# A 0/1 mask for GpSimd: one-byte floats in place of two-byte ones, in a graph attention stack

## The chip, the cores and the metric

The kernel runs on one core of a Trainium2 chip. The metric is the device time of one execution in microseconds (us); the time of a kernel is the median of its runs. In the profile, PE is TensorE (PEld its weight load), DVE is VectorE, ACT is ScalarE, POOL is GpSimd, and SP issues the DMAs.

## The reference

The input is x of 16 graphs x 1024 nodes x 128 features, in float32, and one adjacency matrix of 1024 x 1024 integers for all graphs. Three layers of masked multi-head attention (8 heads of 16) with a feed-forward part follow each other, then one layer in which the score of an edge is a leaky sum of two node values:

```python
def gnn(adj, h, ...):                                # layers 0, 1, 2
    Q, K, V = (h @ Wq), (h @ Wk), (h @ Wv)           # 8 heads of 16
    scores = einsum('bnhd,bmhd->bhnm', Q, K) / sqrt(16)
    scores = where(adj == 0, -inf, scores)
    x = h + einsum('bhnm,bmhd->bnhd', softmax(scores), V) @ Wo + bo
    x = layer_norm(x)
    return layer_norm(x + relu(x @ W1 + b1) @ W2 + b2)

def last(x, adj, ...):                               # layer 3
    h = x @ W
    e = leaky_relu((h @ a_src)[:, :, None] + (h @ a_dst)[:, None, :], 0.2)
    att = nan_to_num(softmax(where(adj == 0, -inf, e)))
    return layer_norm(att @ h + x)
```

## The kernel before

**Blocks and steps.** One block is one graph in one of the three attention layers, 48 in all; graphs go through the layers in groups of four. A block has 32 steps: two groups `g` of four heads, two halves `qh` of 512 query nodes, eight tiles `kt` of 128 key nodes. A step makes the scores of four heads for 128 keys x 512 queries, with keys on the partitions. It takes them in two pairs of heads (`pp` 0 and 1): for each pair PE writes 128 x 1024 scores into a PSUM slot (three slots in all, `s`; L422).

**Two ways to mask.** The scores of a pair become masked exponentials in a tile `e` (six in all) in one of two ways. On the first, ACT takes the exponential from PSUM (L429) and POOL multiplies the result in SBUF, in place, by the 0/1 mask `mask01` (L430). On the second, DVE adds `mask_add`, which holds 0 or -57344 in one-byte floats, to the scores in PSUM (L432), and ACT takes the exponential of that later, in place (L444). The first way is used for the first pair of the steps with `kt` not in (2, 5, 7), so for 5 of 8 steps, 960 times in all; all other pairs, 2112, go the second way.

```python
on_pool = pp == 0 and kt not in BOTH_ON_DVE
m = (mask01 if on_pool else mask_add)[:, kt, q0:q0 + 512][:, None, :].to_broadcast([P, 2, 512])
if on_pool:
    nc.scalar.activation(ev, psv, AF.Exp, scale=HD ** -0.5)
    behind["pool"] = nc.gpsimd.tensor_mul(ev, ev, m).ins
else:
    behind["dve"] = nc.vector.tensor_add(ev, psv, m).ins
```

**Sums.** Four steps later (`AHEAD`) PE multiplies the exponentials by the values, with a column of ones for the sum (L449, eight matmul records a step, into one PSUM accumulator `acc`). After the eight steps of a half, DVE transposes the accumulator (L460) and POOL scales it (L463).

**Around the steps.** Between the steps PE, ACT and DVE work on the next block's projections and on the last block's output projection, feed-forward part and layer norms. POOL has the rest of a layer norm: the small operations on the means and variances (L336 to L338), the scaling of each row tile (L340), gain and bias (L344, L345). The order of PE and ACT is written out by hand, that of DVE and POOL in the main loop comes from the planner of the framework; each engine goes through its list in order and waits on semaphores.

**The masks.** At the start the adjacency rows arrive by DMA as integers, DVE turns them into 0/1 bf16 (L196), PE transposes them into PSUM as bf16 (L202), and `masks()` makes both masks from there: DVE copies to `mask01` (L207), ACT makes `mask_add` (L208). There are eight row tiles. Four are done before the first step, and four in steps 1 to 4, in which the order of DVE is by hand as well.

**The last layer.** For each graph it runs beside later blocks. It reads `mask01` too: in `edges()` DVE takes the maximum of PSUM with 1 and multiplies by the mask in one instruction (L609), 128 times.

## Time and profile before

| | |
|---|---|
| time, median of 3 runs | 4011.02 us (4008.79 to 4011.72) |
| span of the profiled execution | 4007.5 us |
| its time beside the span | not listed apart |
| PE busy | 3767.4 us, 94% |
| DVE busy | 3412.3 us, 85% |
| ACT busy | 3380.2 us, 84% |
| POOL busy | 3450.1 us, 86% |
| mean granted TensorE clock | 0.983 |

A share of busy time is an average over stages. The steady part runs to about 3840 us; each block of attention takes about 73 us there when no last layer runs beside it. The last 150 us are the end of the last graph, with POOL and ACT mostly idle. In the rows of the profile, the number after x counts instructions, then come busy time and mean ns of one, then the idle time of the engine just before them and what ended it. A wait named after a releaser is inferred from semaphore events.

### The profile page before, as it was taken

How to read it: one execution, taken by the hardware profiler on the slowest of the kernel's cores; microseconds unless marked ns; L12 is line 12 of the kernel's file. 1: busy time of each engine (PE TensorE's matmuls, PEld its weight loads, DVE VectorE, ACT ScalarE, POOL GpSimd, SP SyncE). 2: the span in 40 equal slices, each digit the busy share in tenths (PEclk: the TensorE clock that was granted, in tenths of full speed). 3: DMA queues.
4: the chain of work that ended last, by engine and by line, in shares of the span. 5: the costliest groups of instructions: out<-in, count | busy, mean ns of one | idle time of the engine just before them, and what ended most of it. 6: DMA issues, size and time to landing. Idle time of an engine off the chain costs nothing.

```text
span 4007.5 us, 107755 instructions
## 1 busy us (share of the span) xinstructions
PE 3767.4 (94%) x44501; PEld 1551.0 (39%) x44501; DVE 3412.3 (85%) x5326; ACT 3380.2 (84%) x3961; POOL 3450.1 (86%) x3010
## 2 busy tenths in 40 slices
PE   7999999999999999999999999999999999999986
PEld 2333333344443333334444333333444433333435
DVE  7888988988888988988888988988888898988864
ACT  7999999977779999997777999999777799999850
POOL 5889989988889989998788999989888899989884
PEclk8999999999999999999999999999999999999998
DMA  6222122212222222122222222222222121222100
GB/s 162 64 65 59 49 64 65 53 46 67 55 56 59 56 64 64 48 60 55 55 55 55 64 64 57 51 64 65 55 55 55 49 64 49 59 65 62 46 7 20
DMA packets 124465, 233.13 MB, mean 58 GB/s; under 512 B 34624, under 2 KB 73792, under 8 KB 123968
## 3 DMA queue, kind: packets, MB, share of 16 engines
q1 hardware_dynamic: 122960, 225.71, 22.5%
q8 instruction: 354, 5.80, 0.6%
q14 instruction: 143, 1.17, 0.1%
q10 hardware_dynamic: 1008, 0.44, 0.0%
HBM read 15.54 MB, written 8.39 MB: 6 GB/s over the span
## 4 chain that ended last, share of the span: by engine, by line
PE 60%; DVE 17%; POOL 16%; issue 4%; ACT 3%; SPq 1%; DMA 0%; ACTq 0%; DVEq 0%; POOLq 0%
PE acc L449 23%; PE t L296 19%; PE s L422 15%; DVE e L432 10%; POOL e L430 7%; POOL x L344 3%; POOL x L345 3%; DVE st L321 3%; PE t L285 2%; POOL mv L338 1%; DVE x L328 1%; ACT e L444 1%; DVE lo L385 1%; DVE mv L323 1%; POOL x L340 1%
## 5 line engine op out<-in xcount | busy, mean ns | idle before, releaser
L432 DVE TENSOR_TENSOR e<-s,mask_add 128x1024 f32<-128x1024 f32 x2112 | 2492.6, 1213 | 315.1 <-PE s L422 206.5
L444 ACT ACTIVATE e<-e 128x1024 f32<-128x1024 f32 x2112 | 2193.6, 1062 | 197.5 <-DVE e L432 181.6
L430 POOL TENSOR_TENSOR e<-e,mask 128x1024 f32<-128x1024 f32 x960 | 2052.9, 2152 | 343.4 <-ACT e L429 326.9
L449 PE MATMUL acc<-e,v 128*17 128x512 f32 x12288 | 1636.2, 604 | 61.9 <-POOL e L430 30.4
L422 PE MATMUL s<-Wq,Wk 64*128 64x512 f32 x6144 | 1177.0, 455 | 50.1 <-DVE e L432 33.6
L429 ACT ACTIVATE e<-s 128x1024 f32<-128x1024 f32 x960 | 982.9, 1024 | 245.9 <-PE s L422 245.8
L422 PEld LDWEIGHTS s<-Wq,Wk 64*128 64x128 f32 x6144 | 499.3, 186 | 1011.1 <-issue 397.5
L449 PEld LDWEIGHTS acc<-e,v 128*17 128x17 f32 x12288 | 208.0, 95 | 574.1 <-issue 466.9
L340 POOL TENSOR_SCALAR x<-x,mv 128x128 f32<-128x128 f32 x896 | 389.1, 448 | 23.5
L296 PE MATMUL t<-hd,e 128*32 128x129 f32 x8192 | 243.5, 276 | 5.7 <-DVE x L624 3.3
L338 POOL TENSOR_TENSOR mv<-mv,half_neg 128x4 f32<-128x4 f32 x224 | 232.5, 1038 | 18.6
L344 POOL TENSOR_TENSOR x<-x,ln_g 128x1024 f32<-128x1024 f32 (+1 forms) x97 | 229.6, 2367 | 10.3 <-PE t L285 6.3
L296 PEld LDWEIGHTS t<-hd,e 128*32 128x32 f32 x8192 | 226.3, 111 | 23.9 <-DVE lo L385 9.9
L328 DVE TENSOR_TENSOR x<-t,x 128x512 f32<-128x512 f32 x192 | 131.5, 685 | 93.5 <-PE t L296 93.5
L296 PE MATMUL t<-x1T,W 128*32 128x512 f32 x1536 | 200.1, 592 | 1.9 <-DVE x L624 1.0
L321 DVE BATCH_NORM_STATS2 st<-x 128x6 f32<-128x128 f32 x896 | 197.0, 279 | 3.3
L296 PEld LDWEIGHTS t<-W,hT 128*32 128x32 f32 x6144 | 174.0, 111 | 59.9 <-issue 45.5
L296 PE MATMUL t<-W,hT 128*32 128x128 f32 x6144 | 188.1, 275 | 1.8 <-ACT x1T L290 0.9
L285 PEld LDWEIGHTS t<-identf,x 128*128 128x128 f32 x888 | 95.8, 142 | 227.6 <-issue 87.5
L285 PE MATMUL t<-identf,x 128*128 128x128 f32 x888 | 156.0, 291 | 27.0 <-DVE parts L586 7.4
L385 DVE TENSOR_TENSOR lo<-t,hi 128x512 fp32r<-128x512 f32 x188 | 128.2, 682 | 35.6 <-ACT hi L384 35.6
L336 POOL TENSOR_SCALAR mv<-mv 128x4 f32<-128x4 f32 x224 | 53.0, 236 | 122.6 <-DVE mv L323 102.7
(97 smaller groups left out, 2507.7 us busy)
## 6 DMA issues: line engine op xcount, KB each, us to landing
Wk<-hi SPq DMA_DIRECT2D x384, 128.0 KB
Wk<-lo SPq DMA_DIRECT2D x384, 128.0 KB
Wq<-hi SPq DMA_DIRECT2D x384, 128.0 KB
Wq<-lo SPq DMA_DIRECT2D x384, 128.0 KB
x<-in_x_dram SPq DMA_DIRECT2D x16, 512.0 KB
out_dram<-x SPq DMA_DIRECT2D x31, 256.0 KB
ai<-in_adj_dram SPq DMA_DIRECT2D x8, 512.0 KB
g_rows<-parts SPq DMA_DIRECT2D x120, 4.0 KB
```

Of the source, the lines that this page charges most:

```text
L285: nc.tensor.transpose(ps[:, t * P:(t + 1) * P], src[:, 4 * h + t, :], identf)
L296: nc.tensor.matmul(dst[j:j + SLOT, :], lhsT[:, j:j + SLOT], rhs, start=start, stop=stop)
L321: nc.vector.bn_stats(st[:, t, :], z[:, t, :])
L338: nc.gpsimd.tensor_tensor(v, v, half_neg[:, ts], OP.pow)
L340: nc.gpsimd.tensor_scalar(z[:, t, :], z[:, t, :], mv[:, t, 0:1], mv[:, t, 1:2], op0=OP.add, op1=OP.mult)
L344: nc.gpsimd.tensor_mul(z, z, rows(gain, n))
L422: nc.tensor.matmul(ps[:, r * 512:(r + 1) * 512], k[64 * r:64 * r + 64, kt * P:(kt + 1) * P], q[64 * r:64 * r + 64, q0:q0 + 512], start=Tru ...
L429: nc.scalar.activation(ev, psv, AF.Exp, scale=HD ** -0.5)
L430: behind["pool"] = nc.gpsimd.tensor_mul(ev, ev, m).ins
L432: behind["dve"] = nc.vector.tensor_add(ev, psv, m).ins
L444: nc.scalar.activation(ev, ev, AF.Exp, scale=HD ** -0.5)
L449: nc.tensor.matmul(acc[j * SLOT:j * SLOT + HD + 1, :], v_bufs[m % 2][:, kt, 2 * j + g, :], e[:, j, :], start=first, stop=last)
```

## The change

`mask01` is allocated as `float8e5` (the type that `mask_add` has already) in place of bf16, 8 KB instead of 16 KB on each partition; 0 and 1 are exact in both. The copy that fills it gets the flag for a conversion without saturation. The instructions, their order on each engine and the sizes of all pools are the same.

```diff
-    mask01 = const.tile([P, NT, N], BF16)
+    mask01 = const.tile([P, NT, N], F8W)
     mask_add = const.tile([P, NT, N], F8W)
...
     def masks(t, ps):
         psv = ps.rearrange("p (k q) -> p k q", q=P)
-        nc.vector.tensor_copy(mask01[:, :, t * P:(t + 1) * P], psv)
+        nc.vector.tensor_copy(mask01[:, :, t * P:(t + 1) * P], psv, saturate=False)
```

The instructions that touch `mask01` are L207 (8 times, DVE), L430 (960 times, POOL) and L609 (128 times, DVE).

## The prediction

> **What bounds the kernel now.** First the page's busy times, then the windows of two stages (for each engine: busy us, and instructions in brackets).

> ```profile
> PE 3767.4 (94%) x44501; PEld 1551.0 (39%) x44501; DVE 3412.3 (85%) x5326; ACT 3380.2 (84%) x3961; POOL 3450.1 (86%) x3010
> ```

> ```profile
> 418.00:752.00 334.00, 320.94 (x3276) 117.02 (x3278) 298.41 (x437) 315.20 (x358) 305.01 (x260) 1.00 0.23 58
> 1753.00:2086.00 333.00, 315.97 (x4432) 148.06 (x4431) 280.26 (x471) 255.42 (x320) 277.42 (x253) 0.98 0.22 56
> ```

> PE is busy for 321 of 334 us in a stage of attention layers and 316 of 333 where the last layer is mixed in. So PE sets the pace in both. POOL, where the edit lands, has 29 and 56 us free. What counts is how its queue meets PE's, so next the groups of POOL and DVE (count | busy us, mean ns | idle before).

> ```profile
> L430 POOL TENSOR_TENSOR e<-e,mask 128x1024 f32<-128x1024 f32 x960 | 2052.9, 2152 | 343.4 <-ACT e L429 326.9 <-DMA Wk<-lo 11.1 <-DMA ln_gamma<-in_L_gnn_ln_gamma_dram 1.4
> L340 POOL TENSOR_SCALAR x<-x,mv 128x128 f32<-128x128 f32 x896 | 389.1, 448 | 23.5
> L344 POOL TENSOR_TENSOR x<-x,ln_g 128x1024 f32<-128x1024 f32 x95 | 227.1, 2390 | 9.8 <-PE t L285 5.8
> L463 POOL TENSOR_TENSOR A<-tt,recs 128x256 f32<-128x256 f32 x192 | 119.7, 624 | 1.5 <-DVE recs L462 1.5
> L336 POOL TENSOR_SCALAR mv<-mv 128x4 f32<-128x4 f32 x224 | 53.0, 236 | 122.6 <-DVE mv L323 102.7 <-DVE chk L352 4.5
> ...
> L344 POOL TENSOR_TENSOR x<-x,ln_gamma 128x512 f32<-128x512 f32 x32 | 41.1, 1284 | 1.9
> ```

> ```profile
> L432 DVE TENSOR_TENSOR e<-s,mask_add 128x1024 f32<-128x1024 f32 x2112 | 2492.6, 1213 | 315.1 <-PE s L422 206.5 <-ACT e L444 97.6 <-ACT hT L505 0.7
> ...
> L609 DVE SCALAR_TENSOR_TENSOR e<-s,mask 128x1024 f32<-128x1024 f32 x128 | 150.4, 1212 | 4.2 <-PE s L606 3.5
> ...
> L207 DVE COPY mask<-s 128x1024 bf16<-128x1024 bf16 x8 | 5.5, 690 | 4.8 <-PE s L202 4.5
> ```

> The edit touches L430, L609 and L207. Who waits for L430: the list of waits (us in total, times, longest), and one such place in the timeline.

> ```profile
> PEld acc L449 <- POOL e L430: 43.8, 33, 4.5
> ...
> PE acc L449 <- POOL e L430: 30.4, 16, 4.2
> ```

> ```profile
> 1003.29 2.38 POOL L345 TENSOR_TENSOR x<-x,ln_b_last 128x1024 f32<-128x1024 f32 x1
> 1005.62 2.13 POOL L430 TENSOR_TENSOR e<-e,mask 128x1024 f32<-128x1024 f32 x1
> ...
> 1007.81 1.05 PE L449 MATMUL acc<-e,v 128*17 128x512 f32 x8 [2.94 <-POOL e L430]
> ```

> PE itself stands still for L430 only 30.4 us in all. In the place shown, four scale-and-shift instructions precede the one multiplication that PE wants. Over the timeline I set the end of each of the 960 multiplications against the start of its step's L449: the median slack is 4.2 us, a quarter have under 3.4, 57 under 1, 11 under 0.1.

> [...]

> **The change part by part.** No instruction, wait or transfer is added or moved, on any queue; 8 KB a partition come free and no buffer count uses them.

> *L430.* No row of POOL shows a one-byte operand. Fixed cost from the fp32 pair: 1284 - 512 x 2.16 = 178 ns. Per element then: fp32 with fp32 2.16 ns, fp32 with bf16 (2152-178)/1024 = 1.93, fp32 with a scalar repeated 16 times (L463) (624-178)/256 = 1.74. Counted in four-byte words read per element these are 2, 1.5 and 1.06, so a word costs 0.44 to 0.46 ns. With one byte it is 1.25 words: 1.93 - 0.25 x 0.45 = 1.81 ns, 2.04 us in all. That is the value I take, -0.11 us, 106 us less POOL busy. Lower end: the rate of one input, (448-236)/124 = 1.71 ns, gives 1.93 us (-0.22). Upper end: one-byte conversion may cost extra; the nearest price is the fp32 row, 2.39 us (+0.24), and nothing in the profile excludes more.

> What a change d of each is worth in time I work out from the timeline: POOL's lag grows by d with each multiplication, shrinks by its idle time before one that waited for ACT (201 times), and where it exceeds the slack above, PE and all behind it move by the rest; a gain counts only as far as PE really stood still. Result:

> - d = -0.22: -4 us; -0.11: -2.6
> - d = +0.10: +4; +0.12: +7
> - d = +0.24: +56; +0.32: +101; +0.50: +225

> The gain is small because one to three multiplications lie between POOL's last idle time and each stall. The loss is steep because POOL has 29 us for 91 multiplications in the attention stage, 0.32 us each; above d = 0.32 POOL bounds it.

> *L609.* L432 already reads a one-byte mask_add beside PSUM in 1213 ns, L609 a bf16 mask in 1212. Cost: none, both ends within 0.02 us x 128 = 2.6 us.

> *L207.* [...]+0.52 us x 8 = 4.2 us on DVE, and ACT's L208 starts after it. The first four end before 19 us, where PE waits until 24.7 for the DMA of Wq anyway. Of the other four, most go into gaps such as this one, 0.47 of 0.52:

> ```profile
> 35.67 0.69 DVE L207 COPY mask<-s 128x1024 bf16<-128x1024 bf16 x1 [1.13 <-PE s L202]
> ...
> 36.83 1.23 DVE L432 TENSOR_TENSOR e<-s,mask_add 128x1024 f32<-128x1024 f32 x1 [0.47 <-PE s L422]
> ```

> I take +1 us, ends 0 and 4.2; if the cover is gone, all 4.2 show.

> *Sum.* Span 4007.5 - 2.6 + 0 + 1 = 4005.9. The profile gives no total beside the span; the median 4011.0 stands 3.5 above it. Forecast 4009.5, -0.04%, inside the 0.2% (8 us) that a measurement can tell from no change.

> **The rivals.** (1) *POOL pays for one byte.* Place: L430, 960 times; price +0.24 us or more; it decides from 2.27 us on (+0.12, +8 us with L207). At the fp32 price the time is 4011 + 56 + 1 = 4068; at +0.5, 4237. For it: POOL's rate does depend on the type, and one byte is unseen. Against it: the three rates above order by bytes read, the fewer the faster.
> (2) *The gain is on the path.* The chain gives L430 7.2% of the span, 288 us, some 134 multiplications; x 0.11 is -15 us, 3997 with L207. Against it: in the pattern that repeats every block the chain reaches PE through "POOL mv L338" (ended at 494.51 us in one), where DVE's L460, which frees the accumulator, ended at 494.46. There PE waits for L460, not for POOL.
> (3) *Nothing changes on POOL*[...]: 4011 + 1 = 4012, as good as the forecast.

> **How the numbers follow.** Forecast with (3), d between -0.22 and about +0.10: 0.54, own range 4003 to 4017. (1): 0.38, high because nothing measured here excludes it. (2): 0.08. The faster chance is (2), the slower (1). From 4003, some 5% are left below; upward the range takes in the fp32 price and a little (d = 0.28, +80), 4090, leaving about 15% of (1) above.

> **What would show it.** In the changed profile: L430's mean (2.04 right, 2.15 for (3), 2.27 or more for (1)); POOL busy near 3340; PE's wait on L430 within a few us of 30.4 (over 60 means (1)); L207 near 1.2 us; L609 at 1.21. Wrong would be an L430 of unchanged or lower mean with a time over 8 us away: then the slack is misread.

## The result, and the profile after

The changed kernel takes 4003.0 us (median of 13 runs, 4000.31 to 4007.38), the kernel before beside it 4011.7 us (13 runs, 4008.79 to 4018.69). The ratio is 0.998, 95% interval 0.9972 to 0.9988: 8.7 us less. Repeated later with 21 runs it was 4003.97 us and 0.9983 (0.9976 to 0.9989). So the gain is real, though it is just at the 8 us that the prediction took for what a measurement can tell from no change. The time lies 6.5 us below the forecast of 4009.5, at the very lower end of the stated range of 4003 to 4090. The instructions first: busy times, and the chain's shares by engine, from the page of the changed kernel:

```profile
span 4003.6 us, 107755 instructions
PE 3763.0 (94%) x44501; PEld 1552.2 (39%) x44501; DVE 3415.6 (85%) x5326; ACT 3379.7 (84%) x3961; POOL 3333.5 (83%) x3010
PE 64%; DVE 19%; POOL 8%; ACT 5%; issue 3%; SPq 0%; DMA 0%; ACTq 0%; DVEq 0%; POOLq 0%
```

The groups of the edited instructions and of L432 (count | busy us, mean ns | idle before):

```profile
L430 POOL TENSOR_TENSOR e<-e,mask 128x1024 f32<-128x1024 f32 x960 | 1935.7, 2027 | 436.2 <-ACT e L429 436.0
...
L432 DVE TENSOR_TENSOR e<-s,mask_add 128x1024 f32<-128x1024 f32 x2112 | 2492.4, 1213 | 305.5 <-PE s L422 187.2 <-ACT e L444 96.6 <-POOL e L430 8.3
L609 DVE SCALAR_TENSOR_TENSOR e<-s,mask 128x1024 f32<-128x1024 f32 x128 | 150.4, 1212 | 3.6 <-PE s L606 3.1
L207 DVE CAST mask<-s 128x1024 fp8e5<-128x1024 bf16 x8 | 9.8, 1222 | 4.6 <-PE s L202 4.5
```

L430 went from 2152 to 2027 ns, and POOL is busy for 116.6 us less. L609 is unchanged. L207 is now called a CAST and takes 1222 ns instead of 690. All of this is close to what the prediction worked out. Who waits for L430 (us in total, times, longest), from the waits of the changed kernel:

```profile
PEld acc L449 <- POOL e L430: 58.6, 90, 4.0
...
PE acc L449 <- DVE tt L460: 28.3, 50, 1.0
PE acc L449 <- POOL e L430: 23.1, 11, 3.7
PE acc L449 <- POOL x L340: 7.7, 32, 0.3
```

And two of these rows in the kernel before:

```profile
PE acc L449 <- POOL mv L338: 18.2, 32, 0.6
PE acc L449 <- DVE tt L460: 10.5, 40, 0.6
```

PE waits 7.3 us less for L430. But its wait for L460 grew from 10.5 to 28.3 us, and the row of "POOL mv L338" is gone. Most of it is one wait under two names. Set place by place, the 32 waits for L338, 18.2 us in all, are in the changed kernel waits of 18.3 us for L460, and six waits for L430 of 6.0 us in all are six of 6.0 us for L460. One of these is at 1041.6 us, where the kernel before shows a pause of 1.00 us "<-POOL e L430"; the changed kernel shows 0.99 us "<-DVE tt L460" at 1044.1. The group of L449, first in the kernel before and then in the changed one, has the same idle time before it:

```profile
L449 PE MATMUL acc<-e,v 128*17 128x512 f32 x12288 | 1636.2, 604 | 61.9 <-POOL e L430 30.4 <-POOL mv L338 18.2 <-DVE tt L460 10.5
L449 PE MATMUL acc<-e,v 128*17 128x512 f32 x12288 | 1631.5, 603 | 61.5 <-DVE tt L460 28.3 <-POOL e L430 23.1 <-POOL x L340 7.7
```

So PE stands still as long as ever.

That shows in the whole span too: span minus PE's busy time is 4007.5 - 3767.4 = 240.1 us before, and 4003.6 - 3763.0 = 240.6 after. **The time went out of PE's busy time**, with the same 44501 instructions. The windows of the two stages that the prediction showed, for the changed kernel (span, busy us of PE, PEld, DVE, ACT, POOL with instructions, PE clock, DMA share, GB/s):

```profile
418.00:752.00 334.00, 320.89 (x3276) 117.04 (x3272) 298.77 (x437) 314.96 (x357) 293.90 (x260) 1.00 0.23 58
1753.00:2086.00 333.00, 315.54 (x4459) 148.64 (x4459) 283.37 (x476) 258.79 (x324) 272.32 (x256) 0.99 0.22 56
```

The attention stage is as it was, with 11 us less POOL work in its window: from the first L449 of block 15 to that of block 22 both kernels take 512.1 us. The stages in which a last layer runs beside the blocks differ. Blocks 10 to 14, 22 to 26 and 34 to 38 take 466.8, 466.9 and 467.9 us before, and 468.0, 464.2 and 464.0 after: 5.4 us less together, though the first is longer. It is in these stages, and at the end, that the granted clock dips: after the first 50 us it is on record at 0.50 from 843 to 1155 us, from 1822 to 2131, from 2802 to 3109 and from 3781 us on, each time in parts, and once elsewhere, for 3.4 us at 120 in the changed kernel. Here are the two places where both kernels have a pause, first in the timeline of the changed kernel (start, duration, in brackets the idle time before it and what ended that):

```profile
1004.07 2.39 POOL L345 TENSOR_TENSOR x<-x,ln_b_last 128x1024 f32<-128x1024 f32 x1
...
1006.41 2.01 POOL L430 TENSOR_TENSOR e<-e,mask 128x1024 f32<-128x1024 f32 x1
...
1008.48 1.91 PE L449 MATMUL acc<-e,v 128*17 128x512 f32 x8 [2.70 <-POOL e L430]
...
1044.11 1.05 PE L449 MATMUL acc<-e,v 128*17 128x512 f32 x8 [0.99 <-DVE tt L460]
...
1047.05 0.50 PE L422 MATMUL s<-Wq,Wk 64*128 64x512 f32 x2 [0.73 <-DVE e L609]
1047.48 1.05 PE L449 MATMUL acc<-e,v 128*17 128x512 f32 x8
```

And the second place in the timeline of the kernel before:

```profile
1041.63 1.05 PE L449 MATMUL acc<-e,v 128*17 128x512 f32 x8 [1.00 <-POOL e L430]
...
1044.56 0.79 PE L422 MATMUL s<-Wq,Wk 64*128 64x512 f32 x2 [0.73 <-DVE e L609]
1045.28 1.91 PE L449 MATMUL acc<-e,v 128*17 128x512 f32 x8
...
1048.28 1.91 PE L449 MATMUL acc<-e,v 128*17 128x512 f32 x8
```

Eight records of L449 take 1.05 us or 1.91. In the kernel before, the pause of 0.73 us is followed by slow matmuls; in the changed kernel the same pause isn't, while that of 2.70 us is. The windows show the clock in the slow stretches. Kernel before:

```profile
1044.60:1050.20 5.60, 5.60 (x23) 1.14 (x24) 4.52 (x4) 3.02 (x3) 4.24 (x5) 0.50 0.13 33
```

Changed kernel:

```profile
1008.50:1013.40 4.90, 4.90 (x28) 1.20 (x32) 1.58 (x2) 2.28 (x3) 4.90 (x4) 0.50 0.00 0
1044.00:1050.00 6.00, 4.82 (x36) 1.76 (x40) 5.80 (x8) 2.83 (x4) 5.74 (x9) 1.00 0.51 126
```

The granted clock is 0.50 in the slow stretches and 1.00 where the same matmuls are fast. I counted such stretches over the whole timeline (L449's eight records at the slow duration, or a pair of L422 over 0.7 us, gaps under 3 us joined): 21 stretches and 65.8 us before, 16 and 51.3 us after. At half the clock, 14.5 us fewer of them are worth, as an estimate, at most 7.3 us.

The clock records of the traces agree: between 60 and 3880 us they stand at 0.50 for 68.3 us in the kernel before and for 54.6 in the changed one. They also show more than the slow matmuls do. In all 14 traces the clock changes only at the borders of a grid of cells, each 3.413 us long, and the grid lies differently in each execution: its first border in the span is at 0.91, 0.08 and 0.39 us in the three profiles of the changed kernel. Here are four cells of the kernel before, in the order of the windows above:

```profile
1003.21:1006.62 3.41, 1.66 (x32) 0.87 (x24) 2.55 (x3) 2.99 (x6) 3.33 (x3) 1.00 0.52 152
1006.62:1010.04 3.42, 1.71 (x12) 0.43 (x12) 1.79 (x3) 1.76 (x2) 3.42 (x3) 1.00 0.01 2
...
1040.75:1044.17 3.42, 2.19 (x18) 0.93 (x18) 3.24 (x7) 2.89 (x3) 3.07 (x6) 1.00 0.82 195
1044.17:1047.58 3.41, 3.02 (x12) 0.90 (x14) 3.41 (x4) 0.78 (x1) 3.41 (x5) 0.50 0.33 81
```

And two of the changed kernel:

```profile
1004.43:1007.84 3.41, 1.35 (x32) 0.72 (x20) 2.55 (x4) 2.77 (x7) 3.41 (x2) 1.00 0.55 154
1007.84:1011.25 3.41, 2.77 (x12) 0.65 (x12) 1.02 (x1) 1.07 (x2) 3.41 (x4) 0.50 0.00 0
```

The stall of 2.94 us in the kernel before lies across a border: PE is busy for 49% of one cell and 50% of the next, and the clock stays full. The stall of 2.70 us in the changed kernel falls mostly into one cell, in which PE is busy for 40%, and the next cell is at half clock. Nor does the pause of 0.73 us act alone: its cell holds most of the pause of 1.00 us as well, PE is busy for 64% of it, and the clock is halved before the pause of 0.73 us is over. I counted the cells at full clock in the 14 traces from 60 to 3840 us. Of those with PE busy under 45%, all 44 are followed by a cell at half clock; from 45% to 85% it is 102 of 2063; above 85% none of 13209. So in these traces PE's busy share of a cell tells the clock of the next one at both ends; in the middle it does not, and what does stays open. It is partly chance which stalls are followed by half clock in one execution: of the six that are nearly 3 us long, four in the first profile of the kernel before, and three, two and four in the three of the changed one.

### The profile page after: what moved, and what is told of

It reads as the page before. It is cut to its first block, busy times and chain, and to the rows that moved or that the text cites. A ratio compares the mean times of both kernels' runs of the same rounds, so it can differ in the third digit from the quotient of the medians.

```text
span 4003.6 us, 107755 instructions
## 1 busy us (share of the span) xinstructions
PE 3763.0 (94%) x44501; PEld 1552.2 (39%) x44501; DVE 3415.6 (85%) x5326; ACT 3379.7 (84%) x3961; POOL 3333.5 (83%) x3010
## 3 DMA queue, kind: packets, MB, share of 16 engines
q10 hardware_dynamic: 1008, 0.44, 0.1%
## 4 chain that ended last, share of the span: by engine, by line
PE 64%; DVE 19%; POOL 8%; ACT 5%; issue 3%; SPq 0%; DMA 0%; ACTq 0%; DVEq 0%; POOLq 0%
PE acc L449 24%; PE t L296 21%; PE s L422 16%; DVE e L432 10%; POOL e L430 3%; DVE st L321 2%; ACT e L444 2%; PE t L285 2%; POOL x L340 2%; DVE lo L385 2%; ACT e L429 2%; POOL mv L338 1%; DVE x L328 1%; DVE tt L460 1%; POOL x L344 1%
## 5 line engine op out<-in xcount | busy, mean ns | idle before, releaser
L432 DVE TENSOR_TENSOR e<-s,mask_add 128x1024 f32<-128x1024 f32 x2112 | 2492.4, 1213 | 305.5 <-PE s L422 187.2
L444 ACT ACTIVATE e<-e 128x1024 f32<-128x1024 f32 x2112 | 2193.4, 1062 | 194.8 <-DVE e L432 179.3
L430 POOL TENSOR_TENSOR e<-e,mask 128x1024 f32<-128x1024 f32 x960 | 1935.7, 2027 | 436.2 <-ACT e L429 436.0
L449 PE MATMUL acc<-e,v 128*17 128x512 f32 x12288 | 1631.5, 603 | 61.5 <-DVE tt L460 28.3
L422 PE MATMUL s<-Wq,Wk 64*128 64x512 f32 x6144 | 1176.0, 455 | 50.3 <-DVE e L432 35.6
L429 ACT ACTIVATE e<-s 128x1024 f32<-128x1024 f32 x960 | 982.7, 1024 | 242.1 <-PE s L422 242.0
L422 PEld LDWEIGHTS s<-Wq,Wk 64*128 64x128 f32 x6144 | 498.9, 185 | 1009.5 <-issue 396.5
L449 PEld LDWEIGHTS acc<-e,v 128*17 128x17 f32 x12288 | 208.0, 95 | 572.2 <-issue 435.0
L340 POOL TENSOR_SCALAR x<-x,mv 128x128 f32<-128x128 f32 x896 | 389.1, 447 | 23.5
L338 POOL TENSOR_TENSOR mv<-mv,half_neg 128x4 f32<-128x4 f32 x224 | 232.4, 1038 | 18.6
L344 POOL TENSOR_TENSOR x<-x,ln_g 128x1024 f32<-128x1024 f32 (+1 forms) x97 | 229.6, 2367 | 21.8 <-PE t L285 21.8
L285 PEld LDWEIGHTS t<-identf,x 128*128 128x128 f32 x888 | 96.0, 142 | 224.3 <-issue 86.5
L285 PE MATMUL t<-identf,x 128*128 128x128 f32 x888 | 156.2, 292 | 25.6 <-DVE parts L586 7.4
L336 POOL TENSOR_SCALAR mv<-mv 128x4 f32<-128x4 f32 x224 | 53.0, 237 | 129.8 <-DVE mv L323 110.2
```

What stands on the lines that cost most here:

```text
L285: nc.tensor.transpose(ps[:, t * P:(t + 1) * P], src[:, 4 * h + t, :], identf)
L338: nc.gpsimd.tensor_tensor(v, v, half_neg[:, ts], OP.pow)
L340: nc.gpsimd.tensor_scalar(z[:, t, :], z[:, t, :], mv[:, t, 0:1], mv[:, t, 1:2], op0=OP.add, op1=OP.mult)
L344: nc.gpsimd.tensor_mul(z, z, rows(gain, n))
L422: nc.tensor.matmul(ps[:, r * 512:(r + 1) * 512], k[64 * r:64 * r + 64, kt * P:(kt + 1) * P], q[64 * r:64 * r + 64, q0:q0 + 512], start=Tru ...
L444: nc.scalar.activation(ev, ev, AF.Exp, scale=HD ** -0.5)
```

## The experiments

The theory after the result: (A) with the shorter multiplication fewer of PE's pauses bring its clock down, so that the clock is halved for less time. The rivals: (B) the gain is the direct one, PE waiting less for L430; (C) it is not POOL's time at all, but another property of the changed program (the bytes of the mask, the layout of memory, the start). The numbers of stretches below are all counted as above. In the two expectations that come first, "Theory B" is another one: that the number of stretches is chance.

**Profiles of the same two kernels again.**

> The kernel before, profiled a second time. In the two profiles at hand the TensorE matmuls of L449 have two durations, 0.60 and 1.03 us, and the long ones come in stretches of 3 to 6 us after PE stood still: 21 stretches (66 us in all) before, 16 (51 us) after the change. Theory A (the stretches follow POOL's stalls, which the shorter multiplication removes): this profile has them where the first one had, about 66 us in all, and stalls of 2.9 us at L449 near 1008, 1109, 1987, 2966 and 3066 us. Theory B (their number is chance): it differs from the first by as much as the changed kernel did, 5 stretches or 15 us.

> The changed kernel, profiled a second time. Theory A: about 51 us in slow stretches again, at the same places, L430 at 2.03 us, and the stretches of attention layers alone exactly as long as before. Theory B: another number of slow stretches, as far from 51 us as 66 us is.

Measured: the kernel before has a span of 4009.4 us, PE busy 3768.0, 21 stretches, 69.9 us. The changed kernel has 4003.6 us, PE busy 3762.0, 16 stretches, 51.4 us. So the difference lies between the kernels and not between two executions, though the places of the stretches, which the expectations took for fixed, differ from one execution to the next. Where both kernels have the stall behind the four scale-and-shift instructions, it is about 2.95 us before and 2.70 after; it occurs six times.

**POOL's time put back, the one-byte mask kept.** Each multiplication is issued as two of 512, one for each head:

```
-behind["pool"] = nc.gpsimd.tensor_mul(ev, ev, m).ins
+for c in (slice(0, 1), slice(1, 2)):
+    behind["pool"] = nc.gpsimd.tensor_mul(ev[:, c], ev[:, c], m[:, c]).ins
```

> The one-byte mask kept, but each multiplication of L430 is issued as two of 512 elements, one for each head of the pair. By the fixed cost of 0.18 us and an overlap of 0.05 us that puts POOL's time for a pair back to about 2.11 us from one start to the next, what it is with the bf16 mask (2.10). Theory A (the gain is POOL's shorter multiplication): the gain is gone, 4011 to 4018 us. Rival (the gain comes from something else that goes with the type: other addresses in SBUF, DVE's reads, the order of the first microseconds): 4001 to 4006 us, as the changed kernel.

Measured: 4010.37 us, ratio 1.000 (0.9992 to 1.0009). The group of L430 and the page's busy times:

```profile
PE 3779.5 (94%) x44501; PEld 1554.4 (39%) x44501; DVE 3415.1 (85%) x5326; ACT 3381.9 (84%) x3961; POOL 3473.3 (87%) x3970
...
L430 POOL TENSOR_TENSOR e<-e,mask 128x512 f32<-128x512 f32 x1920 | 2074.7, 1109 | 329.0 <-ACT e L429 328.1
```

POOL's multiplications take 2074.7 us, about as much as before (2052.9), and the gain is gone, with 21 stretches and 68.2 us. That speaks against (C), with two reservations. The order on POOL changes a little, where an L463 falls between the halves. And PE's busy time is 12 us above that of the kernel before, its idle time 8 below, so the sum is back but not by the same parts.

**DVE's copy at the start doubled**, on the kernel before:

```
-nc.vector.tensor_copy(mask01[:, :, t * P:(t + 1) * P], psv)
+for _ in range(2):
+    nc.vector.tensor_copy(mask01[:, :, t * P:(t + 1) * P], psv)
```

> The bf16 mask kept, but the copy L207 that fills it is issued twice, so that DVE spends 1.3 us on each row tile in place of 0.69 (the conversion to one byte takes 1.22). It is the cost of the edit without its gain. If the first microseconds cost what the two profiles show (first L449 0.9 us later), the time is 4012 to 4014 us, +1 to +2. Rival (all eight show): +5 us, 4016.

Measured: 4009.09 us, ratio 0.9996 (0.9987 to 1.0004). The first L449 starts at 45.6 us against 43.8 in the kernel before, and nothing of these 1.8 us can be told in the time. The longer L207 neither costs nor brings anything that this measurement sees.

**The slope on the slow side**: the kernel before, with L430 in three parts.

```
+for c, w in ((0, slice(0, 512)), (1, slice(0, 256)), (1, slice(256, 512))):
+    behind["pool"] = nc.gpsimd.tensor_mul(ev[:, c, w], ev[:, c, w], m[:, c, w]).ins
```

> The bf16 mask kept, each multiplication of L430 issued in three parts (512, 256 and 256 elements). By the fixed cost of 0.18 us and an overlap of 0.05 us, POOL takes some 2.36 us for a pair from one start to the next in place of 2.10, d = +0.26. It tests the price of the prediction's first rival, the slope on the slow side. By the slack counted in the profile before (+56 at 0.24, +90 at 0.30) the time is about 4011 + 65 = 4076, with L449's waits on L430 grown from 30 us to nearly 100. Rival reading (POOL has more room than the slack says, since all else shifts with PE): 4025 to 4045. If slow clock stretches come on top: 4090 or more.

Measured: 4068.59 us (4 runs), ratio 1.0143 (1.0128 to 1.0158), which is 51 to 63 us more. Its waits for L430, and the window of an attention stage:

```profile
PEld acc L449 <- POOL e L430: 122.9, 209, 4.6
```

```profile
1260.00:1846.00 586.00, 563.00 (x5690) 206.03 (x5682) 512.77 (x753) 545.61 (x624) 570.95 (x750) 1.00 0.22 55
```

From the first L449 of block 15 to that of block 22 it takes 522.0 us instead of 512.1, at full clock. POOL is busy for 571 of the 586 us shown, more than PE: there it is close to being the bound. The group's busy time grew by (2328.6 - 2052.9)/960 = 0.29 us per multiplication. The slack counting of the prediction gave +56 us at 0.24 and +101 at 0.32, which is about +84 at 0.29 on a straight line. So the loss is steep, as predicted, but only some two thirds of what was counted.

**Half of POOL's work left out.** The one-byte kernel multiplies only the first head of the pair; the mask of the second is left out.

```
+behind["pool"] = nc.gpsimd.tensor_mul(ev[:, :1], ev[:, :1], m[:, :1]).ins
```

> The one-byte mask kept, but only the first head of each pair is multiplied by it; the mask of the second is left out. L430 takes 1.1 us in place of 2.03, and the order on every engine stays. If POOL's time is what PE waits for, all waits of L449 on L430 but the part due to the four scale-and-shift instructions ahead of it go: of nine stalls of 2.7 us each about 0.9 us goes, and with them some slow clock stretches: 3985 to 3998 us. Rival (the first 0.12 us took all that was to be had): 4001 to 4004.

Measured: 3972.98 us (4 runs), ratio 0.9909 (0.9895 to 0.9924), below what was expected. PE waits for L430 5.2 us instead of 23.1. Span minus PE's busy time is 223.1 us, 17.5 below the changed kernel, and busy time is down by 14.0, with 9 stretches and 22.3 us. So of the 31.5 us in the span a little over half is standing still and the rest is busy time. Not all of PE's idle time depends on POOL: 223 us remain.

**The stall taken away.** In blocks 12 to 14, 24 to 26 and 36 to 38 the first pair of step 19, which waits behind the scale-and-shift instructions, is masked by DVE. The edit is made to the one-byte kernel and to the kernel before:

```
-on_pool = pp == 0 and kt not in BOTH_ON_DVE
+on_pool = pp == 0 and kt not in BOTH_ON_DVE and (
+    step[0] < 12 or step[0] % 12 > 2 or 16 * g + 8 * qh + kt != 19)
```

> The one-byte mask kept; in nine blocks (12 to 14, 24 to 26, 36 to 38) the first pair of step 19 is masked by DVE in place of POOL, nine multiplications of 960. Those are the ones that stand behind four scale-and-shift instructions in POOL's queue and for which PE stands still 2.7 us. Theory (the loss sits in those places): 6 to 9 stalls of 2.7 us go, 16 to 24 us, and some slow stretches: 3975 to 3988 us. Rival (DVE is then late by its 1.2 us there, or L449 waits for the next multiplication in the same queue): 3996 to 4003.

> The bf16 mask with the same nine pairs masked by DVE. If the gain of the one-byte mask lies in those stalls and the slow stretches behind them, it is gone where they are gone: within 3 us of the same edit with the one-byte mask. Rival (it lies elsewhere in the stages with a last layer): 7 to 10 us above it.

Measured: 3984.13 us (3977.25 to 3991.11), ratio 0.9934 (0.9922 to 0.9946), with one byte, and 3987.39 us (3982.35 to 3997.52), ratio 0.9949 (0.9934 to 0.9963), with two. The waits of the one-byte kernel, and the place of the 2.70 us in its timeline:

```profile
PE acc L449 <- POOL e L430: 5.3, 6, 3.7
```

```profile
1010.15 1.05 PE L449 MATMUL acc<-e,v 128*17 128x512 f32 x8 [0.33 <-POOL e L430]
```

The pause is 0.33 us and no half clock follows it. The one-byte version has 12 stretches and 30.9 us, that with two bytes 11 and 25.3. Nine multiplications of 960 moved to another engine bring more than twice what the shorter 960 brought: 18.9 us, about 10 in standing still (span minus busy 230.2) and 7.5 in busy time. Between the two masks 3.3 us are left where 8.7 were; the intervals overlap, so that most of the change's gain lies in these places is likely but not shown.

**A seventh tile `e`**, with the one-byte mask (the freed memory has room for it):

```
-tag="e", name="e", bufs=6
+tag="e", name="e", bufs=7     # and the same for the other user of this tag
```

> The one-byte mask, and the 8 KB a partition that it frees spent on a seventh tile e. Every order stays. The profile shows no wait for a free tile e among its larger waits, so 4001 to 4006 us as the changed kernel. Rival (ACT and DVE are held back by the six tiles where POOL is late): 3990 to 3998.

Measured: 4010.19 us (13 runs), ratio 0.9999 (0.999 to 1.0007). The page and the group:

```profile
PE 3767.2 (94%) x44501; PEld 1547.4 (39%) x44501; DVE 3413.5 (85%) x5326; ACT 3385.1 (85%) x3961; POOL 3333.8 (83%) x3010
...
L430 POOL TENSOR_TENSOR e<-e,mask 128x1024 f32<-128x1024 f32 x960 | 1935.8, 2027 | 442.2 <-ACT e L429 428.5
```

This is the run that limits the explanation. The multiplication is as short as in the changed kernel, PE stands still a little less (238.0 us), and yet the gain is gone: 22 stretches, 68.8 us, PE busy 3767.2. A short L430 alone is therefore not enough. The seventh tile takes 4 x 512 float32, 8 KB a partition, which is just what the mask had freed. So this run does not exclude rival (C), a layout of the memory that matters; no run changed the layout alone. Why a seventh tile brings the slow stretches back stays open.

**The best version, and the tile on top of it.** To the nine places a tenth is added, the first pair of step 16 of block 47, and in the second kernel the seventh tile:

```
 on_pool = ... and step != (47, 0, 1, 0)
```

> As the kernel with nine pairs moved to DVE, with one more: the first pair of step 16 of the last block (47), for which PE stands still 3.7 us near the end, behind two scale-and-shift instructions. If that stall is on the path: 3 to 5 us below 3984, 3978 to 3982. Rival (the end of the kernel waits for something else): 3982 to 3986.

> Ten pairs on DVE and seven tiles e, the best version if both help. If the seventh tile does nothing: 3978 to 3984 as the kernel with ten pairs. Rival: 5 us or more below it, because DVE's moved pairs hold a tile longer.

Measured: 3981.23 us, ratio 0.9929 (0.9916 to 0.9943), and 3981.59 us, ratio 0.9928 (0.9915 to 0.9942). The busy times and the wait of the first:

```profile
PE 3749.4 (94%) x44501; PEld 1549.3 (39%) x44501; DVE 3424.8 (86%) x5336; ACT 3379.0 (85%) x3961; POOL 3314.1 (83%) x3000
```

```profile
PE acc L449 <- POOL e L430: 2.5, 6, 1.1
```

Both beat the changed kernel by over 21 us, with 22.2 and 27.6 us of stretches. What the tenth place adds to the nine (3984.13 us) cannot be told: the intervals overlap. With the long stalls gone, the seventh tile costs nothing and brings nothing.

**The changed kernel a third time, with more runs.**

> The changed kernel itself, timed again beside the kernel before. The seven-tile version has the same short L430 (2.03 us) and the same shorter stalls, but 69 us of slow clock stretches and no gain (4010). If the changed kernel's 4003 is a property of it: 4001 to 4006 again, with about 51 us of slow stretches, and the seventh tile then costs the gain by where its pauses fall. If it was a property of the chip or the day: 4008 to 4012, with 60 to 70 us of slow stretches.

Measured: 4003.97 us, ratio 0.9983 (0.9976 to 0.9989); in the profile span 4000.1 us, PE busy 3758.4, span minus busy 241.7, 15 stretches, 39.8 us.

Put side by side, the profiled executions give this table:

| kernel | span | PE busy | span - busy | slow stretches, us |
|---|---|---|---|---|
| before | 4007.5, 4009.4 | 3767.4, 3768.0 | 240.1, 241.4 | 65.8, 69.9 |
| DVE's copy doubled | 4007.6 | 3765.2 | 242.4 | 61.2 |
| changed | 4003.6, 4003.6, 4000.1 | 3763.0, 3762.0, 3758.4 | 240.6, 241.6, 241.7 | 51.3, 51.4, 39.8 |
| changed, seven tiles | 4005.2 | 3767.2 | 238.0 | 68.8 |
| changed, nine on DVE | 3985.7 | 3755.5 | 230.2 | 30.9 |
| before, nine on DVE | 3983.6 | 3752.0 | 231.6 | 25.3 |
| changed, ten on DVE | 3977.8 | 3749.4 | 228.4 | 22.2 |
| changed, ten, seven tiles | 3983.1 | 3753.2 | 229.9 | 27.6 |
| changed, half multiplied | 3972.1 | 3749.0 | 223.1 | 22.3 |
| changed, in two parts | 4011.6 | 3779.5 | 232.1 | 68.2 |
| before, in three parts | 4076.2 | 3831.0 | 245.2 | 75.1 |

In all rows but the last two a straight line through PE's busy time against the time in slow stretches fits within 2 us: 0.38 us of busy time for each us in them. The two kernels that issue the multiplication in parts lie above that line, by 11 and 60 us. Nearly all of that is in L449, busy for 1646.5 and 1699.0 us against 1636.2 before, while the mean of one record is 604 and 605 ns against 604. Its matmuls are not slower there, they overlap less. Short waits inside a group of eight would look like this; that was not followed up. Where the kernel before and the changed one differ, all of it is in the column of PE busy: means of 3767.7 and 3761.1, 6.6 us, against spans of 4008.5 and 4002.4, 6.0 us.

The mean granted clock is on record for every run, not only for the profiled ones, and this says more than the profiles. Here is the mean span in us of the runs with the same clock, with the number of runs in brackets: the kernel before in the four batches of the experiments (78 runs), and the changed kernel in two (34 runs).

| mean granted clock | before | changed |
|---|---|---|
| 0.981 | 4014.8 (5) | |
| 0.982 | 4010.8 (36) | 4006.2 (1) |
| 0.983 | 4008.1 (29) | 4007.8 (4) |
| 0.984 | 4005.2 (5) | 4004.0 (9) |
| 0.985 | 4002.6 (3) | 4001.4 (9) |
| 0.986 | | 3999.4 (11) |

Within one and the same kernel, runs with a lower clock are longer, and at the same clock the two kernels are about 1 us apart (1.1 us with a standard error of 0.5, from a fit with one slope for both), while their means differ by 7.0 us. So about six of seven us go with the clock: the changed kernel has more runs with a high one.

So (B) falls as the source of most of the gain: the direct wait became shorter by about 0.25 us six times, but PE's idle time didn't. That the gain goes with the clock is shown, by profiles and runs alike, though only as an association: no experiment set the clock. That it was the shorter L430 which spared the clock is less sure. The run in two parts speaks for it, and the run with seven tiles shows that it is not enough.

## Why the prediction was right, and where a size was off

The range held only just: 4003.0 is its lower end, below which the prediction had left some 5%, and the repeat gave 4003.97. L430's mean and that of L609 came out by the reasons given, that of L207 as estimated, and PE stands still about as long as before, as forecast. That a gain of 8.7 us, most of it from a source that the prediction did not count, still lay inside is luck.

- **L430**: 2.04 us was worked out from the bytes read, 2027 ns was measured. With the 178 ns taken off, that is 1.81 ns an element, as forecast. (The rows before give 0.43 to 0.46 ns for a word, not 0.44 to 0.46; the result is the same.) The 2.16 ns an element of two fp32 inputs are (2390 - 1284)/512, from L344 with 1024 and with 512 elements. No extra cost of the one-byte operand can be seen: the 2.04 us were worked out without one, and 2027 ns is no more.
- **POOL busy**: about 3340 forecast, 3333.5 measured.
- **L609 and L207**: as forecast. L609 has a mean of 1212 ns before and after. L207 went from 690 to 1222 ns, +0.53 us; the +0.52 of the forecast is the 1213 ns of L432 less 690. That a copy into one byte takes as long as L432 was an estimate, and why it takes longer than one into two bytes was not shown.
- **The start**: +1 us taken. The first L449 starts at 44.5 to 45.2 us in three profiles, against 43.8 and 43.9 before; with the copy doubled no cost could be told.
- **The rivals**: (1), that POOL pays for one byte, did not occur. Where POOL was slowed by other means, by 0.29 us, it cost 51 to 63 us, less than the 84 or so of the counting. (3) falls with L430's mean. (2), the gain on the path, came as near in time, with 3997 worked out, but not by its reason: the chain's share of L430 fell from 7% to 3% and that of POOL from 16% to 8%, 8% of 4003.6 us or 320 us, while the time fell by 8.7. What the prediction held against it was right: there another engine was as late, and the 32 waits "for L338" are now waits for L460, as long as before.
- **The term that was mis-sized: the gain, "-0.11: -2.6".** The sum counted how long PE stands still. At each long stall that part came as counted, about 0.25 us less; in the total PE's idle time did not shrink. What it left out is that PE's clock is not given: after some pauses the records of L449 take 1.91 us in place of 1.05. At the same clock the two kernels are about 1 us apart, and some 6 us of the gain go with the clock. The clock of 0.98 in the window of the mixed stage, against 1.00 in the attention stage, was in the lines that the prediction showed and was not priced; it is 0.99 after.
- The sentence on what would be wrong named a time over 8 us away with an L430 of unchanged or lower mean. From the forecast it is 6.5, so by this sign the slack was read well enough; from the kernel before it is 8.7.

## What to carry to other kernels

When an engine off the path gets faster, count what its consumer stands still, and then look at the consumer's own clock: a pause that costs little by itself can be followed by matmuls that take nearly twice as long, here 1.91 us in place of 1.05. Where the clock differs from run to run, as here from 0.981 to 0.985 in the kernel before, compare the times at the same clock over many runs; one profile of each kernel does not tell its share. Look for the few places where work for the critical engine queues behind long work of another kind; moving nine instructions out of such places was worth 18.9 us, shortening 960 only 8.7. The price of POOL's two-input operations followed the bytes read per element: with 178 ns taken off, 2.16 ns for eight bytes (L344), 1.93 for six and 1.81 for five (L430 before and after). And a chain of waits that names an engine does not say that a faster engine shortens it: here the chain's share of POOL became some 320 us smaller, and the time fell by 8.7.
